# Two sparse graph-attention layers: another order of the first tiles' work, and edge places on GpSimd instead of VectorE

## The chip, the cores and the metric

The kernel runs on one core of a Trainium2 chip. The metric is the device time of one execution in microseconds. PE is TensorE, PEld its weight load, DVE VectorE, ACT ScalarE, POOL GpSimd and SP the engine that queues the plain DMAs. All times in this text are microseconds unless marked ns.

## The reference

Two graph-attention layers on 3327 nodes with 1024 features. `adj` is a symmetric 0/1 matrix with ones on its diagonal, with about 17 entries to a row. Cut to what matters:

```
# layer 0: 8 heads of 128
h = (x @ W).reshape(C, 8, 128)
e = leaky_relu(alpha_src[i] + alpha_dst[j], 0.2)      # alpha_* = sum over d of h * a_*
attn = softmax(where(adj == 0, -inf, e))              # over j
x = layernorm(x + attn @ h)
# layer 1: one head of 1024, the same form with W, a1, a2, and relu on its output
x = layernorm(x + relu(attn1 @ (x @ W1)))
```

## The kernel before

**Three stages.** Nodes are cut into 26 tiles of 128 rows (`NT`). The first part, which is all that the change touches, makes the features of layer 0 and turns the adjacency matrix into lists of edges. Then layer 0 gathers rows of `h0_d` by those lists, tile by tile, and layer 1 does the same with `y_d`. Between the first part and layer 0 a flag is computed that chooses the sparse branch; it needs the counts of all 26 tiles, so no gather starts before the first part is over.

**Features.** `flip(t)` transposes a tile of x on PE (L176) and copies it out on ACT (L179, two copies). `project(t, c)` multiplies it by the third `c` of W (8 values of k, each one product of fp32 in two passes, L480), and `keep(t, c)` copies the sum out on ACT (L497). The three thirds are 347, 347 and 346 columns wide. The last 16 columns of W are "W a", W times the attention vectors: they lie in third 2, so `project(t, 2)` needs them, and thirds 0 and 1 don't. For third 2, `keep` also makes `sd`, `r` and two exponentials on ACT (L492 to L495), and four small operations on POOL (`factors`, L296 to L299). The accumulators have two PSUM banks ("A"), so a project waits until the keep of the one two places before it has been done.

**W a.** `score_column(k)` makes it for rows 128k of W: products of W with `a_src` on DVE (L576) and with `a_dst` on POOL (L575), a sum over each head for the first on DVE (L577), and for the second either 8 sums on ACT (L582, columns 0 to 4) or one on DVE (L579, columns 5 to 7). The vectors reach all partitions by products with a row of ones (L560); the POOL's copy `av` is made from that by ACT (L563). The product tiles `pr0` and `pr1` have two buffers each.

**Edge lists.** For each tile:
- `count(t)`: POOL clears the diagonal in the mask (L308), ACT counts it (`junk`, L311), DVE packs its bytes (`words`, L318). Then POOL queues the load of a later mask. There are four mask buffers; `load_mask(t + 4)` takes the one that this very count reads, so that DMA waits on POOL's queue until the count is over.
- `ends` and `ends2`: a one-column product on PE (L327, L346), a copy on ACT (L328, L347), small operations on POOL (L335 to L353).
- `keys` and `columns`, in two halves each: DVE finds the 32 largest keys (L360, L274, L276) and unpacks them (L369 to L376), giving `pack`.
- `places`: ACT makes `away` (L385, L386); DVE casts `pack` to bf16, takes the remainder (L389, L390) and compares `away` with the degrees (L392, L393), which gives `place`.
- `give(0)` to `give(4)`: groups of small bf16 products on PE, with `place` as weights (L412, L402).
- `take`: six copies on ACT (L424 to L429). `sources`: DVE finds the gathered row of each place (L437 to L451).

**The order of the work** is written out by hand. `listing()` is a generator: each step emits one piece of list work. For tile t it yields four steps (`give(s)` of tile t with a half of `keys` or `columns` of tile t + 1), one step with `give(4)`, `take` and `count(t + 4)`, one with `sources`, and one with `places(t + 1)`, which is held back until third 2 of tile t + 1 has been kept. `pace()` is called after every second k of a project; it counts slots and emits as many steps as the ratio `7 * (NT + 1)` to `slots[1]` asks for. Before, 189 steps go to 284 slots, and a tile has 12 slots: a little under 8 steps for each tile of features, where 7 are a tile of lists. So the lists start behind and catch up. The main loop for t from 2 does `project(t, 0)`, `project(t, 1)`, `flip(t + 2)`, `project(t + 1, 2)`. Every engine runs its instructions in the order in which they were emitted.

```
while done[0] * slots[1] < slots[0] * (7 * (NT + 1)):
    done[0] += 1
    next(steps, None)
```

Of the kernel before, what the change touches and what calls it, by code (L numbers as in the profile page):

```python
# [26 lines left out]
def kernel(  # L27
# [125 lines left out]
    def spread(dst, a):  # L153

        nc.sync.dma_start(dst, bass.AP(tensor=a.tensor, offset=a.offset, ap=[[0, P], [1, D]]))

    class Phase:
# [74 lines left out]
        def edge_constants(self):  # L232
            self.io_w = self.iota([P, WD], [[1, WD]], "io_w")

            self.io_q = self.iota([P, EB * P], [[2 * P, EB], [2, P // 8], [P // 4, 8]], "io_q", base=1)
            part = self.pool.tile([P, 3, NB], I32, bufs=1, name="part")
            nc.gpsimd.iota(part[:, 0, NB - 1 :], pattern=[[0, 1]], base=0, channel_multiplier=1)
            for b in range(EB):
                for g in range(NG):
                    nc.gpsimd.iota(  # L240
                        part[:, 0, b * NG + g : b * NG + g + 1], pattern=[[0, 1]], base=(b + g) % EB * P,
                        channel_multiplier=1,
                    )
            nc.vector.tensor_scalar(
                part[:, 1, :], part[:, 0, :], 7, 4, op0=OP.bitwise_and, op1=OP.logical_shift_left
            )
            nc.vector.tensor_scalar(
                part[:, 2, :], part[:, 0, :], 3, 15, op0=OP.logical_shift_right, op1=OP.bitwise_and
            )

            nums = self.pool.tile([P, 1], I32, bufs=1, name="nums")
            nc.vector.tensor_scalar(nums, part[:, 0, NB - 1 :], GT - 1, None, op0=OP.bitwise_and)
            self.mvs = [self.pool.tile([P, 3, NY], BF16, bufs=1, name=f"mvs{n}") for n in range(4)]
            for mv in self.mvs:
                nc.vector.memset(mv, 0.0)
                nc.vector.tensor_scalar(mv[:, 0, :1], nums, 1.0, None, op0=OP.add)
                nc.vector.tensor_scalar(mv[:, 0, NY - 1 :], part[:, 0, NB - 1 :], 1.0, None, op0=OP.add)
            nc.vector.tensor_scalar(part[:, 0, :], part[:, 0, :], -P, None, op0=OP.bitwise_and)
            for n in range(2):
                nc.vector.tensor_tensor(part[:, 0, :], part[:, 0, :], part[:, n + 1, :], OP.bitwise_or)  # L260
            self.io_k = self.pool.tile([P, NB], F32, bufs=1, name="io_k")
            nc.vector.tensor_copy(self.io_k, part[:, 0, :])
            self.io_l = self.iota([P, KMAX], [[1, KMAX]], "io_l")
            self.bit = self.pool.tile([P, 8, KMAX], I32, bufs=1, name="bit")
            self.base = self.pool.tile([P, 8, KMAX], F32, bufs=1, name="base")
            for b in range(8):
                first = (b & 1) * NP // 2 + (b >> 1 & 1) * NP // 4 + (b >> 2) * NP // 8 + 1
                nc.vector.memset(self.bit[:, b, :], 1 << b)
                nc.vector.memset(self.base[:, b, :], float(first))

        def largest(self, dst, src, half):
# [8 lines left out]
    class Edges:  # L280
# [83 lines left out]
        def columns(self, half):  # L364

            sbuf, ph = self.ph.sbuf, self.ph
            if half == 0:
                ki = sbuf("ki", [P, 3, KMAX], 1, dt=I32)
                nc.vector.tensor_copy(ki[:, 0, :], self.top)  # L369
                nc.vector.tensor_scalar(ki[:, 1, :], ki[:, 0, :], 9, None, op0=OP.logical_shift_right)  # L370
                nc.vector.tensor_scalar(ki[:, 2, :], ki[:, 0, :], 511, None, op0=OP.bitwise_and)
                bits = sbuf("bits", [P, 8, KMAX], 1, dt=I32)
                nc.vector.tensor_tensor(bits, ki[:, 1:2, :].to_broadcast([P, 8, KMAX]), ph.bit, OP.bitwise_and)
                self.cols = sbuf("cols", [P, 8, KMAX], 1)
                nc.vector.tensor_tensor(self.cols, ki[:, 2:3, :].to_broadcast([P, 8, KMAX]), ph.base, OP.add)
                nc.vector.scalar_tensor_tensor(self.cols, bits, 0.0, self.cols, op0=OP.not_equal, op1=OP.mult)  # L376
                self.pack = sbuf("pack", [P, KMAX], 1)
            ph.largest(self.pack, self.cols.rearrange("p a b -> p (a b)"), half)

        def places(self):  # L380
# [5 lines left out]
            nc.scalar.activation(away[:, EB * P :], ph.io_q[:, :P], AF.Abs, bias=self.mid2, scale=-1.0)  # L386

            mv = self.mv = ph.mvs[self.t % 4]
            nc.vector.tensor_copy(mv[:, 0, XL:NX], pack)  # L389
            nc.vector.tensor_tensor(mv[:, 1, XL:NX], pack, mv[:, 0, XL:NX], OP.subtract)  # L390
            self.place = sbuf("place", [P, (EB + 1) * P], 2, dt=BF16)
            nc.vector.tensor_scalar(self.place[:, : EB * P], away[:, : EB * P], self.deg, None, op0=OP.is_lt)  # L392
            nc.vector.tensor_scalar(self.place[:, EB * P :], away[:, EB * P :], self.more, None, op0=OP.is_lt)  # L393

        def give(self, b):

# [35 lines left out]
        def sources(self):  # L432
# [1 line left out]
            sbuf, ph, t = self.ph.sbuf, self.ph, self.t  # L434
            xv, m = self.xs, NB - 1
            kq = sbuf("kq", [P, NB], 1)
            nc.vector.tensor_tensor(kq[:, :m], ph.io_k[:, :m], xv[:, :m, 0], OP.subtract)  # L437
            nc.vector.tensor_tensor(kq[:, m:], ph.io_k[:, m:], xv[:, m, KMAX + 1 :], OP.subtract)
            eq = sbuf("eq", [P, NB, KMAX], 1)
            nc.vector.tensor_tensor(  # L440
                eq, ph.io_l.unsqueeze(1).to_broadcast([P, NB, KMAX]),
# [12 lines left out]
    with ExitStack() as own, tc.manual_schedule():  # L454
# [47 lines left out]
        def count(t):  # L502
            if t < NT:
                lists[t].words(ads.pop(t), junk)
                load_mask(t + 4)

        def listing():

            for t in range(-1, NT):
                old, new = lists[t] if t >= 0 else None, lists[t + 1] if t + 1 < NT else None  # L510
                for s in range(4):
                    if old:
                        old.give(s)
                    if new:
                        (new.keys, new.columns)[s // 2](s % 2)
                    if s == 1 and t + 3 < NT:
                        lists[t + 3].ends(tri_b)
                    if s == 3 and t + 3 < NT:
                        lists[t + 3].ends2(all_b)
                    yield  # L520
                if old:
# [26 lines left out]
        arow = [pool.tile([1, D], F32, bufs=1, name=f"arow{n}") for n in range(2)]  # L548
        for n, a in enumerate((a0_src, a0_dst)):
            nc.sync.dma_start(arow[n], bass.AP(tensor=a.tensor, offset=a.offset, ap=[[D, 1], [1, D]]))  # L550
        for k in range(KT):
            nc.sync.dma_start(wt[:, k, :D], w0[k * P : (k + 1) * P, :])
            if k == 3:
                load_x(1)
        one = pool.tile([1, P], F32, bufs=1, name="one")
        nc.vector.memset(one, 1.0)
        avs = bank("S", [P, NG, HALF], "avs")
        for n in range(4):
            half = slice(n % 2 * HALF, (n % 2 + 1) * HALF)
            nc.tensor.matmul(avs[:, n, :], one, arow[n // 2][:, half], start=True, stop=True)  # L560
        av = pool.tile([P, D], F32, bufs=1, name="av")
        for n in range(2):
            nc.scalar.activation(av[:, n * HALF : (n + 1) * HALF], avs[:, 2 + n, :], AF.Copy)  # L563
        masks = [pool.tile([P, NP], U8, bufs=1, name=f"ad{n}") for n in range(5)]
        for ad in masks[:4]:
            nc.vector.memset(ad[:, N:], 0.0)
# [4 lines left out]
        def score_column(k):  # L571
            pr = [ph.sbuf(f"pr{n}", [P, D], 2) for n in range(2)]
            to = [wt[:, k, D + n * H : D + (n + 1) * H] for n in range(2)]
            heads = [pr[n].rearrange("p (h d) -> p h d", h=H) for n in range(2)]
            nc.gpsimd.tensor_tensor(pr[1], wt[:, k, :D], av, OP.mult)  # L575
            nc.vector.tensor_tensor(pr[0], wt[:, k, :D], avs[:, :2, :].rearrange("p a b -> p (a b)"), OP.mult)  # L576
            nc.vector.tensor_reduce(to[0], heads[0], AX.X, OP.add)  # L577
            if k > 4:
                nc.vector.tensor_reduce(to[1], heads[1], AX.X, OP.add)  # L579
                return  # L580
            for h in range(H):
                nc.scalar.activation(junk_h, heads[1][:, h, :], AF.Copy, accum_out=to[1][:, h : h + 1])  # L582

        flip(0)
        for k in range(3):
            score_column(k)
        load_mask(0)
        project(0, 0, False)
        keep(0, 0)
        flip(1)  # L590
        load_x(2)
        score_column(3)
        project(0, 1, False)
        keep(0, 1)
        score_column(4)
        load_mask(1)
        project(1, 0, False)
        for k in range(5, KT):
            score_column(k)
        keep(1, 0)  # L600
        project(1, 1, False)
        keep(1, 1)

        tri = pool.tile([P, P], F32, bufs=1, name="tri")
        nc.vector.memset(tri, 0.0)
# [4 lines left out]
        )  # L610
        tri_b = pool.tile([P, P], BF16, bufs=1, name="tri_b")
        nc.vector.tensor_copy(tri_b, tri)
        count(0)
        ph.edge_constants()

        nc.vector.memset(tri, 1.0)
# [2 lines left out]
        )  # L619
        all_b = pool.tile([P, P], BF16, bufs=1, name="all_b")  # L620
        nc.vector.tensor_copy(all_b, tri)
        lists[0].ends(tri_b)
        lists[0].ends2(all_b)
        load_mask(2)
        count(1)
        flip(2)
        load_x(3)
        slots[1] = (NT - 2) * 12 - 4
        project(0, 2, False)
        keep(0, 2)  # L630
        load_mask(3)
        count(2)
        lists[1].ends(tri_b)
        lists[1].ends2(all_b)
        flip(3)
        load_x(4)
        project(1, 2)
        keep(1, 2)
        project(2, 2)
        keep(2, 2)  # L640
        for t in range(2, NT):
            load_x(t + 3)
            if 4 <= t < 4 + KT:
                nc.sync.dma_start(wt1[:, t - 4, :], w1[(t - 4) * P : (t - 3) * P, :])
# [567 lines left out]
```

## Time and profile before

| | us |
|---|---|
| median of 10 runs (1908.44 to 1914.04) | 1911.33 |
| the profiled execution, its own time | 1915.67 |
| its span, first to last instruction | 1913.6 |
| PE busy over the span | 1512.4 |
| last product of the first part ends | 490 |
| first gather of layer 0 is issued | 497 |
| first gather of layer 1 is waited for | 1217 |

The profile's 40 slices are 47.8 us each, so the first part fills the first ten and a half. In a timeline line the columns are start, duration, engine, source line, operation, output and inputs, sizes and how many were merged; the bracket gives the idle time before it and who ended it. In a table of waits the columns are the total in us, how often, and the longest. A pass of a 128x346 product takes 0.295 us when PE runs without gaps, so a project of 16 passes takes 4.73.

### The profile page before, as it was taken

How to read it: one execution, taken by the hardware profiler on the slowest of the kernel's cores; microseconds unless marked ns; L12 is line 12 of the kernel's file. 1: busy time of each engine (PE TensorE's matmuls, PEld its weight loads, DVE VectorE, ACT ScalarE, POOL GpSimd, SP SyncE). 2: the span in 40 equal slices, each digit the busy share in tenths (PEclk: the TensorE clock that was granted, in tenths of full speed). 3: DMA queues.
4: the chain of work that ended last, by engine and by line, in shares of the span. 5: the costliest groups of instructions: out<-in, count | busy, mean ns of one | idle time of the engine just before them, and what ended most of it. 6: DMA issues, size and time to landing. Idle time of an engine off the chain costs nothing.

```text
span 1913.6 us, 38096 instructions
## 1 busy us (share of the span) xinstructions
PE 1512.4 (79%) x14663; PEld 897.7 (47%) x14663; DVE 1148.4 (60%) x3083; ACT 545.4 (29%) x1408; POOL 1038.7 (54%) x1393
## 2 busy tenths in 40 slices
PE   6699999999456566555566555399999999999997
PEld 3455555666345455454455544134444444444443
DVE  5599999888287566666566666344444444444442
ACT  5355554442112222222222222012221222222210
POOL 4322222211466667676676664577766676666650
PEclk9799999999668877787778878699999999999999
DMA  5655565411699999999999998799999999999980
GB/s 151 98 122 111 119 111 99 97 61 50 227 392 372 398 393 400 374 405 400 392 383 393 398 387 299 286 395 409 404 385 371 388 374 369 358 371 374 372 336 33
DMA packets 170923, 567.22 MB, mean 296 GB/s; under 512 B 27674, under 2 KB 34330, under 8 KB 170734
## 3 DMA queue, kind: packets, MB, share of 16 engines
q0 software_dynamic: 131056, 455.68, 67.3%
q1 hardware_dynamic: 39678, 109.04, 15.0%
q8 instruction: 117, 1.92, 0.4%
q14 instruction: 72, 0.59, 0.1%
HBM read 578.33 MB, written 42.97 MB: 325 GB/s over the span
## 4 chain that ended last, share of the span: by engine, by line
PE 54%; DMA 23%; DVE 11%; ACT 6%; issue 4%; POOL 3%; DVEq 0%; ACTq 0%; SPq 0%; POOLq 0%
DMA src<-h_d,idx 21%; PE mm L1005 19%; PE mm L480 13%; PE acc L973 12%; DVE e L850 3%; PE tr L176 3%; PE acc L878 3%; ACT junk L311 2%; POOL src L783 2%; DVE pr L911 1%; ACT xT L179 1%; PE acc L862 1%; DMA src<-y_d,idx 1%; PE xp L412 1%; DMA own<-h_d 1%
## 5 line engine op out<-in xcount | busy, mean ns | idle before, releaser
L783 POOL DMA_INDIRECT src<-h_d,idx x416 | 442.2, 1063 | 205.0 <-PE acc L878 60.1
L783 POOL DMA_INDIRECT src<-y_d,idx x416 | 416.5, 1001 | 221.3 <-PE acc L973 95.0
L878 PE MATMUL acc<-src,e 128*32 128x128 f32 x6656 | 275.9, 335 | 255.2 <-DVE e L850 254.9
L480 PE MATMUL mm<-wt,xT 128*128 128x347 f32 (+1 forms) x1248 | 399.2, 466 | 3.0 <-ACT xT L179 2.2
L1005 PE MATMUL mm<-wt,xT 128*128 128x512 f32 x832 | 381.6, 602 | 0.8 <-DVE o L1008 0.8
L878 PEld LDWEIGHTS acc<-src,e 128*32 128x32 f32 x6656 | 232.1, 136 | 313.9 <-DVE e L850 286.8
L480 PEld LDWEIGHTS mm<-wt,xT 128*128 128x128 f32 x1248 | 227.7, 192 | 106.3 <-ACT xT L179 3.0
L1005 PEld LDWEIGHTS mm<-wt,xT 128*128 128x128 f32 x832 | 151.6, 189 | 198.4 <-issue 178.0
L973 PE MATMUL acc<-src,es 128*32 128x342 f32 (+1 forms) x2496 | 205.7, 463 | 34.1 <-DVE es L964 32.3
L850 DVE TENSOR_TENSOR e<-oh,way 128x1024 f32<-128x1024 f32 x130 | 158.8, 1221 | 59.2 <-ACT w L848 58.8
L973 PEld LDWEIGHTS acc<-src,es 128*32 128x32 f32 x2496 | 71.5, 111 | 158.6 <-issue 113.1
L848 ACT ACTIVATE w<-way 128x32 f32<-128x32 f32 (+1 forms) x130 | 24.7, 190 | 402.5 <-DVE way L846 390.9
L1008 DVE SCALAR_TENSOR_TENSOR o<-mm,y 128x512 f32<-128x512 f32 x52 | 36.0, 692 | 163.6 <-PE mm L1005 163.6
L987 ACT ACTIVATE z<-y,ri 128x342 f32<-128x342 f32 (+1 forms) x78 | 39.5, 569 | 313.4 <-DVE ri L983 313.4
L845 DVE TENSOR_TENSOR way<-src,re 128x32 f32<-128x32 f32 x104 | 20.9, 201 | 175.1 <-DMA src<-h_d,idx 154.9
L179 ACT ACTIVATE xT<-tr 128x512 f32<-128x512 f32 x104 | 59.4, 595 | 140.4 <-PE tr L176 140.4
L961 DVE TENSOR_TENSOR way<-way,src 128x128 f32<-128x128 f32 x104 | 31.1, 299 | 95.0 <-DMA src<-y_d,idx 51.0
L311 ACT ACTIVATE junk<-ad 128x3328 uint8<-128x3328 uint8 x26 | 78.3, 3013 | 11.1 <-POOL ad L308 11.1
L830 ACT ACTIVATE own<-own,es 128x128 f32<-128x128 f32 x208 | 63.6, 388 | 59.7 <-DVE es L827 59.7
L862 PE MATMUL acc<-end,e 128*128 128x128 f32 x416 | 64.8, 319 | 13.6 <-DVE e L850 13.6
L870 PE MATMUL acc<-own,ident 128*128 128x512 f32 x104 | 62.0, 680 | 8.5 <-ACT own L830 8.5
L862 PEld LDWEIGHTS acc<-end,e 128*128 128x128 f32 x416 | 59.8, 229 | 15.9 <-DVE e L850 15.9
(190 smaller groups left out, 1857.4 us busy)
## 6 DMA issues: line engine op xcount, KB each, us to landing
h_d<-ht SPq DMA_DIRECT2D x26, 520.0 KB
own<-h_d SPq DMA_DIRECT2D x26, 520.0 KB
y_d<-y SPq DMA_DIRECT2D x26, 514.0 KB
y<-y_d SPq DMA_DIRECT2D x26, 514.0 KB
x<-in_x_dram SPq DMA_DIRECT2D x25, 512.0 KB
y<-in_x_dram SPq DMA_DIRECT2D x25, 512.0 KB
out_dram<-o SPq DMA_DIRECT2D x25, 512.0 KB
ad<-in_adj_dram POOLq DMA_DIRECT2D x25, 415.9 KB
```

What stands on the lines that cost most here:

```text
L176: nc.tensor.transpose(tr[:, k, :], src[:, (4 * g + k) * P : (4 * g + k + 1) * P], ident)
L179: nc.scalar.activation(part, tr, AF.Copy)
L311: nc.scalar.activation(junk, ad, AF.Copy, accum_out=self.deg)
L480: nc.tensor.matmul(acc, xT[t][:, k, :], wt[:, k, CUTS0[c] : CUTS0[c + 1]], start=k == 0, stop=k == KT - 1)
L783: nc.gpsimd.indirect_dma_start(out=s[:, g, :w], out_offset=None, in_=table[:, :], in_offset=bass.IndirectOffsetOnAxis(ap=idx[:, t, b * NG ...
L830: nc.scalar.activation(hn, hn, AF.Copy, scale=es[:, n : n + 1])
L850: nc.vector.tensor_tensor(e, oh.unsqueeze(2).to_broadcast([P, ng, H, wide]), wp.unsqueeze(3).to_broadcast([P, ng, H, wide]), OP.mult,)
L862: nc.tensor.matmul(self.acc[h // 4][:, h % 4, :], e[:, 0, h, :], rowsof[:, 0, h, :], start=False, stop=h % 4 == 3,)
L870: nc.tensor.matmul(self.acc[b - 1].rearrange("p h d -> p (h d)"), ident, self.h[:, (b - 1) * HALF : b * HALF], start=False, stop=False,)
L878: nc.tensor.matmul(self.acc[h // 4][g * GT : (g + 1) * GT, h % 4, :], e[:, g, h, :], rowsof[:, g, h, :], start=first and h % 4 == 0, stop= ...
L973: nc.tensor.matmul(self.acc[c][to, :m], es[:, g, :], s[:, g, CUTS[c] : CUTS[c + 1]], start=b == 0, stop=b == EB,)
L1005: nc.tensor.matmul(acc, xT[:, k, :], wt1[:, k, half], start=k == 0, stop=k == KT - 1)
```

## The change

All edits lie in the first part; layers 0 and 1 are not touched.

- **Start.** x tiles 1 to 4 are loaded a little earlier. `av` is loaded by a DMA that repeats one row to all partitions, ahead of W, and no longer copied by ACT. Columns 0 to 5 of W a have their second product on POOL and their second sums on ACT; columns 6 and 7 have both on DVE, which reads both vectors from PSUM.
- **Order of the first tiles.** Thirds 0 and 1 of tiles 0, 1 and 2 are done while W a is made, and then thirds 2. The constants for the edges now come ahead of `count(0)`. `keys` and `columns` of tile 0 are emitted between the projects, and the pacing starts with 4 steps done at slot 9, with 189 steps to 289 slots.
- **Masks.** `count(t)` now queues `load_mask(t + 3)`, into the buffer that the count before has read.
- **Places on POOL.** The cast and the remainder of `pack`, both comparisons that make `place`, and the two subtractions at the head of `sources` move from DVE to POOL. `pack` gets a second buffer.
- **Unpacking.** The bit masks are shifted by 9, so one DVE operation of `columns` goes.

```
-                nc.vector.memset(self.bit[:, b, :], 1 << b)
+                nc.vector.memset(self.bit[:, b, :], 512 << b)
...
             mv = self.mv = ph.mvs[self.t % 4]
-            nc.vector.tensor_copy(mv[:, 0, XL:NX], pack)
-            nc.vector.tensor_tensor(mv[:, 1, XL:NX], pack, mv[:, 0, XL:NX], OP.subtract)
+            nc.gpsimd.tensor_copy(mv[:, 0, XL:NX], pack)
+            nc.gpsimd.tensor_tensor(mv[:, 1, XL:NX], pack, mv[:, 0, XL:NX], OP.subtract)
...
-            nc.vector.tensor_scalar(self.place[:, : EB * P], away[:, : EB * P], self.deg, None, op0=OP.is_lt)
-            nc.vector.tensor_scalar(self.place[:, EB * P :], away[:, EB * P :], self.more, None, op0=OP.is_lt)
+            nc.gpsimd.tensor_scalar(self.place[:, : EB * P], away[:, : EB * P], self.deg, None, op0=OP.is_lt)
+            nc.gpsimd.tensor_scalar(self.place[:, EB * P :], away[:, EB * P :], self.more, None, op0=OP.is_lt)
...
-            nc.vector.tensor_tensor(kq[:, :m], ph.io_k[:, :m], xv[:, :m, 0], OP.subtract)
-            nc.vector.tensor_tensor(kq[:, m:], ph.io_k[:, m:], xv[:, m, KMAX + 1 :], OP.subtract)
+            nc.gpsimd.tensor_tensor(kq[:, :m], ph.io_k[:, :m], xv[:, :m, 0], OP.subtract)
+            nc.gpsimd.tensor_tensor(kq[:, m:], ph.io_k[:, m:], xv[:, m, KMAX + 1 :], OP.subtract)
...
             lists[t].words(ads.pop(t), junk)
-                load_mask(t + 4)
+                load_mask(t + 3)
```

The order of the first tiles, after the change (without the constants):

```
flip(0); score_column(0); score_column(1); load_mask(0)
project(0, 0, False); keep(0, 0); flip(1); load_x(3)
score_column(2); project(0, 1, False); keep(0, 1); score_column(3); load_mask(1)
project(1, 0, False); keep(1, 0); flip(2); load_x(4)
score_column(4); project(1, 1, False); keep(1, 1); score_column(5); load_mask(2)
project(2, 0, False); keep(2, 0); score_column(6); score_column(7)
...
count(0); next(steps); next(steps)
project(2, 1, False); keep(2, 1); project(0, 2, False); keep(0, 2)
lists[0].ends(tri_b); count(1); next(steps); next(steps)
project(1, 2, False); keep(1, 2)
lists[0].ends2(all_b); lists[1].ends(tri_b); count(2); flip(3); load_x(5)
done[0], slots[:] = 4, [9, (NT - 3) * 12 + 13]
project(2, 2); keep(2, 2); lists[1].ends2(all_b); lists[2].ends(tri_b)
flip(4); project(3, 2); keep(3, 2); lists[2].ends2(all_b)
for t in range(3, NT): ...
```

At the first slot of `project(2, 2)` the pacing emits three steps at once: `count(3)`, `places(0)`, and `give(0)` of tile 0 with a half of `keys(1)`. The order before:

```
flip(0); score_column(0); score_column(1); score_column(2); load_mask(0)
project(0, 0, False); keep(0, 0); flip(1); load_x(2)
score_column(3); project(0, 1, False); keep(0, 1); score_column(4); load_mask(1)
project(1, 0, False); score_column(5); score_column(6); score_column(7); keep(1, 0)
project(1, 1, False); keep(1, 1)
...
count(0)
...
lists[0].ends(tri_b); lists[0].ends2(all_b); load_mask(2); count(1); flip(2); load_x(3)
slots[1] = (NT - 2) * 12 - 4
project(0, 2, False); keep(0, 2); load_mask(3); count(2)
lists[1].ends(tri_b); lists[1].ends2(all_b); flip(3); load_x(4)
project(1, 2); keep(1, 2); project(2, 2); keep(2, 2)
for t in range(2, NT): ...
```

## The prediction

> **What bounds the kernel now.** I read the page's slices first.
>
> ```profile
> span 1913.6 us, 38096 instructions
> ...
> PE   6699999999456566555566555399999999999997
> ...
> DVE  5599999888287566666566666344444444444442
> ...
> PEclk9799999999668877787778878699999999999999
> ```
>
> The change touches only the first ten slices. There PE stands at 9 from the third slice on, and DVE at 8 to 9: one of the two, or a chain through both, sets the pace. PE's products are the same before and after, so I account for PE's lost time: idle, or at half clock. The timeline of PE at the start:
>
> ```profile
> 26.76 9.61 PE L480 MATMUL mm<-wt,xT 128*128 128x347 f32 x32 [2.21 <-ACT xT L179]
> 46.18 0.16 PE L327 MATMUL op<-deg_b,tri_b 128*128 128x1 bf16 x1 [9.81 <-ACT deg_b L313]
> 55.20 0.16 PE L346 MATMUL op<-more_b,all_b 128*128 128x1 bf16 x1 [8.86 <-POOL more_b L340]
> 55.30 1.94 PE L176 MATMUL tr<-ident,x 128*128 128x128 f32 x8
> 57.03 5.82 PE L480 MATMUL mm<-wt,xT 128*128 128x346 f32 x16
> ...
> 70.61 0.16 PE L346 MATMUL op<-more_b,all_b 128*128 128x1 bf16 x1 [7.76 <-POOL more_b L340]
> ...
> 72.45 4.31 PE L480 MATMUL mm<-wt,xT 128*128 128x346 f32 x8
> ...
> 86.60 0.24 PE L412 MATMUL xp<-mvs,place 32*128 32x42 bf16 x12 [0.30 <-DVE place L392]
> ```
>
> Lost here: 2.2 at 24.6; 18.8 from 36.4 to 55.2; 7.8 from 62.9 to 70.6. After each long gap PE runs slowly: transposes take 1.94 where 1.04 is usual, 16 passes 5.82 for 4.73, 8 passes 4.2 for 2.36: 2.0 and 2.8 lost. Sum 33.6.
>
> Then the waits from 80 to 330:
>
> ```profile
> PEld L412 <- DVE place L392: 18.2, 13, 2.1
> PE xp L412 <- DVE place L392: 9.5, 10, 1.5
> ...
> DVE place L392 <- ACT away L385: 5.8, 9, 2.3
> ...
> PE xp L412 <- POOL mvs L299: 1.5, 1, 1.5
> ...
> PE mm L480 <- ACT ht L497: 0.8, 2, 0.4
> ```
>
> PE's own waits are 9.5 + 1.5 + 0.8 = 11.8, nearly all at `give(0)`, for `place`. From 330 on PE has none (40.00 busy of 40). Is DVE the late one? One turn of the timeline says mostly no:
>
> ```profile
> 188.41 0.22 PE L402 MATMUL xp<-mvs,place 128*128 128x43 bf16 x3
> ...
> 189.62 3.02 ACT L311 ACTIVATE junk<-ad 128x3328 uint8<-128x3328 uint8 x1
> ...
> 192.87 0.17 ACT L492 ACTIVATE sd<-mm 128x16 f32<-128x16 f32 x1
> ...
> 193.62 0.73 ACT L385 ACTIVATE away<-io_q,place_of 128x512 f32<-128x512 f32 x1
> ...
> 194.39 0.48 DVE L392 TENSOR_SCALAR place<-away,cnt 128x512 bf16<-128x512 f32 x1 [0.74 <-ACT away L385]
> ...
> 194.93 0.24 PE L412 MATMUL xp<-mvs,place 32*128 32x42 bf16 x12 [1.53 <-DVE place L392]
> ```
>
> It is a loop: `give(4)` on PE, the copies and the 3 us count on ACT, whatever keep stands between, `away`, the comparison, `give(0)`. DVE itself waited 0.74 for `away`. So total lost before: 33.6 + 11.8 = 45.4.
>
> [...] the product of 128x1024 takes 2.37 on POOL (L575) and 1.21 on DVE (L576). It shows no large one-input comparison. [...] Here a small POOL cast (L296), 0.19 to 0.21 elsewhere, took 0.60 at 86.69 beside the two-input key operation of DVE. [...]
>
> **The change part by part.**
>
> *Start, up to W a.* ACT's queue decides. Its first copy is done at 14.3. A column's eight sums take 3.48 (15.37 to 18.81), a keep of a third 0.45, a pair of xT copies 1.07. Columns 0 and 1, keep, xT, column 2, keep, column 3 end at about 30.3; the next keep waits for PE till 31.1 (I grant PE 1.5 lost: `av` puts 0.5 MB ahead of W, and POOL, freed from waiting for ACT's `av`, issues the first mask's load near 13 instead of 21, beside W). Then keep, xT and column 4 end at 36.6, keep and column 5 at 40.8. DVE does columns 0 to 5 in 2.39 each from 12, but in column 6 its second product needs the `pr1` buffer of column 4, which ACT reads until 36.6, and in column 7 that of column 5. Each product or sum is 1.21: W a is ready at 45.0, against 41.5 before. Meanwhile PE has seven projects to do and isn't held: they end at 46.3, `project(0, 2)` at 51.1.
>
> *Constants and first count.* In the trace before, the stretch from the first table cast (47.33) to the end of the second triangle on POOL (53.80) is 6.5; with 1.6 ahead, and 0.3 for the diagonal, the count of tile 0 can start 8.4 after W a. It lasts 3.3 (42.82 to 46.13). So `deg_b` of tile 0 comes at 45.0 + 11.7 = 56.7. `keep(2, 1)` is queued behind that count, and `project(1, 2)` needs its bank: PE idles from 51.1 to 57.2, 6.1.
>
> *From there to the first `give(0)`* everything is a chain through ACT and POOL: keep(2, 1), keep(0, 2) and a copy 1.75; `ends` 1.75; diagonal 0.35; count 1 3.3; sd and r 0.45; factors 1.1; `ends2` 1.15; `ends` 1.5; diagonal 0.35; count 2 3.3; xT 1.1; count 3 3.3; away 0.75; comparison 0.8. Sum 21.0: `give(0)` at 77.7. PE's order puts only `project(1, 2)`, a flip and two products in front of it. Lost: 1.0 slow, 1.0 waiting for count 1, 0.5 slow, 11.3 idle, 2.2 slow afterwards (before: 2.0 and 2.8). Start in all: 1.5 + 6.1 + 1.0 + 1.0 + 0.5 + 11.3 + 2.2 = 23.6, against 33.6. Gain 10.0.
>
> *Places on POOL.* DVE loses 0.37 + 0.79 + 0.33 a tile of lists, and 0.17 by the unpacking. It took 15.5 a tile (from one `re` store to the next), so it falls to 13.9, under the 14.7 that pacing gives (7 steps are 10.7 slots, of 12 to a tile of 16.5). That removes DVE's share of PE's waits. But the ACT chain stays, and its end gets longer. The comparison of 128x512 on POOL: [...] I take 0.68, against 0.51 on DVE. [...] Where third 2 is kept between, POOL does the four factors first (1.5 after r), then cast and remainder (0.55), then compares. The mask's DMA, which held POOL's queue until the count was over, no longer does: without that edit these would queue behind it. The subtractions for `sources` now wait on POOL's queue for `take`; behind them stand only the factors and places of the next tile, which come later anyway.
>
> *PE's waits, counted.* With T the start of `give(4)`: `away` starts at T + 4.45 with no keep between, + 4.79 with one, + 5.75 with keep and xT, + 5.21 with third 2 (all read from the timeline). `place` follows 1.30 later on DVE, 1.50 on POOL; with third 2 on POOL at T + 7.29. PE arrives at T + 4.96 after 8 products, 6.15 after 10, 7.34 after 12; with a flip, 5.86 and 7.05. On the order of before this rule gives 8.8, against 11.0 measured for `give(0)`; the rest is DVE. On the order after, tile by tile: 2 with third 2 and 8 products, 2.33 each; 5 with third 2 and 10, 1.14; 2 with xT and 8, 1.39; 3 with xT and 10, 0.20; 1 with a keep and 8, 1.33; 3 with a keep and 10, 0.14; 2 with none and 8, 0.99; 1 with none, 8 and a flip, 0.09; the last two, without a count, 0.6 each. Sum 18.8. The new ratio, 189 to 289, also ends the catching up at tile 20 instead of 15, so the waits last longer. Loss against 11.8: 7.0.
>
> *Tail.* The last `give(4)` ends the projects as before; the subtractions on POOL add 0.4 (two of 0.2 and a hop). DMAs: masks and x are loaded tiles ahead, nothing waits.
>
> **Sum.** 23.6 + 18.8 = 42.4 for 45.4, and 0.4: -2.6. Span 1913.6 - 2.6 = 1911.0, own time 1915.67 - 2.6 = 1913.1; the median was 4.3 below that execution, 1911.33, so 1908.7: 1909.
>
> **Rivals.**
> *DVE was the bound* (faster). DVE stands at 9 in these slices, and PE's waits name it. If POOL's end of the loop costs no more than DVE's (0.5, and POOL's factors overlap the count), the rule gives 10.0 instead of 18.8: -11.4, 1900. For it: DVE's 94% busy. Against: DVE waited for `away` 9 times of 16.
> *POOL's comparison is the new wait* (slower). It stands between `away` and `give(0)`, and above 0.75 PE waits for it in 24 of 25 tiles, so each 0.1 costs about 2.4. At 1.07 the waits are 28, and the kernel +6.8: 1918. It decides from 0.79 (level with before); at 0.95 the kernel is slower by 0.2%. [...] For it: [...] the 0.60 cast. Against: at that moment DVE should be in MAX8, beside which POOL's operations keep to 0.19.
> *The start gains nothing*: had the chain to `give(0)` 10 more, the end would be +7.4, 1919; every row in it is measured, so I give it little.
>
> **How the numbers follow.** A measurement here tells about 0.2%, 3.8 us, from no change. The forecast's case, 1904 to 1914, has 0.45; the faster rival 0.27; the slower, with the dearer start, 0.28. Within the forecast's case some 0.17 lies beyond -3.8 and 0.03 beyond +3.8: faster 0.44, same 0.25, slower 0.31. The range runs from 1899 to 1921.
>
> **What would show it.** W a ready near 45 with DVE waiting on ACT's sums; first `give(0)` near 78; PE's waits for `place` near 19 in all, released by POOL; a comparison of 0.68; no wait of PE on DVE. Wrong if `give(0)` comes before 73 or after 83, or the comparison is below 0.5 or above 0.95.

## The result, and the profile after

| | before | after |
|---|---|---|
| median of the runs | 1911.73 (28 runs) | 1958.94 (8 runs, 1956.25 to 1962.35) |
| the profiled execution, its own time | 1915.67 | 1957.88 |
| its span | 1913.6 | 1955.4 |
| W a ready | 41.5 | 50.0 |
| first `give(0)` | 86.6 | 83.8 |
| waits of PE for `place` at `give(0)` from there on (without the first `give(0)` itself) | 9.2 in 9 | 45.5 in 25 |
| mean of a pass of features from there on | 0.3184 | 0.3351 |
| start of the last feature product (below: the mark) | 489.5 | 536.8 |

After against before the ratio is 1.0246 (95% interval 1.0237 to 1.0255): 47 us slower. The forecast was 1909, in a range that ended at 1921. The two marks differ by 47.3, so the whole loss lies in the first part; layers 0 and 1 took 5.5 less in the profiled execution of after (span less mark is 1418.6 against 1424.1).

The same slices as before, from the page of the changed kernel:

```profile
span 1955.4 us, 38076 instructions
...
PE   8688989989936666555556655389999999999997
...
DVE  4677777876538666666666665434444444444442
...
PEclk9799989999967888777788887689999999999999
```

The reader is to see three things. DVE has fallen from 8 and 9 to mostly 7 in slices 3 to 10, as the change means it to. PE has not risen with it: it has an 8 in places where there were only nines. And the first part fills eleven slices, not ten. So relieving DVE did not quicken PE.

The start on PE, from the timeline, and after it the waits from 80 to 330:

```profile
18.77 0.85 PE L479 MATMUL mm<-wt,xT 128*128 128x347 f32 x2 [0.43 <-DMA wt<-in_L_gnn_W_dram]
22.91 1.53 PE L479 MATMUL mm<-wt,xT 128*128 128x347 f32 x2 [3.29 <-DMA wt<-in_L_gnn_W_dram]
...
61.62 0.16 PE L327 MATMUL op<-deg_b,tri_b 128*128 128x1 bf16 x1 [5.05 <-ACT deg_b L313]
...
70.24 1.09 PE L176 MATMUL tr<-ident,x 128*128 128x128 f32 x8 [1.02 <-ACT cnt L328]
```

```profile
PEld L411 <- POOL place L391: 46.8, 14, 11.9
...
DVE wd L318 <- POOL ad L308: 43.6, 12, 10.1
PE xp L411 <- POOL place L391: 39.1, 14, 11.3
...
POOL place L391 <- ACT away L384: 32.8, 9, 4.4
...
DVE eq L439 <- POOL kq L437: 14.5, 9, 4.5
```

Where there stood `PE xp L412 <- DVE place L392: 9.5` there is now POOL, with 39.1. Two waits of DVE on POOL have grown: for the diagonal (L308) from 5.4 in one to 43.6 in 12, and for `kq` (the output of the two subtractions) from nothing to 14.5. What POOL needs for the comparison is in the view of its line:

```profile
L391 POOL TENSOR_SCALAR place<-away,cnt x26: 1561/1576/2116, 81.7 to 527.1; 128x512 bf16<-128x512 f32 x26
...
  PE xp L411: 56.8, 26
```

Minimum, median and maximum are in ns: 1.58 us, where I had taken 0.68 and, in the dearest case that I priced, 1.07. PE waited for it in all 26 tiles.

How the 47.3 add up: the first `give(0)` comes 2.8 earlier; the waits behind it grow by 45.5 - 9.2 = 36.3; the passes behind it take 373.7 - 359.2 = 14.5 more, though 12 fewer are left to do there; what remains is -0.7.

### The profile page after: what moved, and what is told of

Same layout as the page of the kernel before. It is cut to its first block, busy times and chain, and to the rows that moved or that the text cites. A ratio compares the mean times of both kernels' runs of the same rounds, so it can differ in the third digit from the quotient of the medians.

```text
span 1955.4 us, 38076 instructions
## 1 busy us (share of the span) xinstructions
PE 1533.4 (78%) x14663; PEld 906.4 (46%) x14663; DVE 1119.0 (57%) x2902; ACT 546.7 (28%) x1422; POOL 1119.6 (57%) x1547
## 4 chain that ended last, share of the span: by engine, by line
PE 51%; DMA 22%; ACT 8%; DVE 8%; POOL 6%; issue 4%; DVEq 0%; POOLq 0%; ACTq 0%; SPq 0%
DMA src<-h_d,idx 20%; PE mm L1023 19%; PE acc L991 12%; PE mm L479 11%; ACT junk L311 4%; DVE e L868 3%; PE acc L896 3%; PE tr L176 2%; POOL place L391 2%; POOL src L801 2%; DVE pr L929 1%; ACT xT L179 1%; PE acc L880 1%; DMA wt<-in_L_gnn_W_dram 1%; PE xp L411 1%
## 5 line engine op out<-in xcount | busy, mean ns | idle before, releaser
L479 PE MATMUL mm<-wt,xT 128*128 128x347 f32 (+1 forms) x1248 | 419.9, 484 | 4.4 <-DMA wt<-in_L_gnn_W_dram 3.7
L479 PEld LDWEIGHTS mm<-wt,xT 128*128 128x128 f32 x1248 | 236.5, 199 | 119.5 <-issue 15.3
L1023 PEld LDWEIGHTS mm<-wt,xT 128*128 128x128 f32 x832 | 151.6, 189 | 198.4 <-issue 178.0
L991 PE MATMUL acc<-src,es 128*32 128x342 f32 (+1 forms) x2496 | 207.0, 465 | 32.1 <-DVE es L982 32.1
L991 PEld LDWEIGHTS acc<-src,es 128*32 128x32 f32 x2496 | 71.7, 111 | 157.0 <-issue 113.3
L391 POOL TENSOR_SCALAR place<-away,cnt 128x512 bf16<-128x512 f32 x26 | 43.0, 1655 | 48.6 <-ACT away L384 48.6
```

Source lines behind the costliest of these rows:

```text
L391: nc.gpsimd.tensor_scalar(self.place[:, : EB * P], away[:, : EB * P], self.deg, None, op0=OP.is_lt)
L479: nc.tensor.matmul(acc, xT[t][:, k, :], wt[:, k, CUTS0[c] : CUTS0[c + 1]], start=k == 0, stop=k == KT - 1)
L991: nc.tensor.matmul(self.acc[c][to, :m], es[:, g, :], s[:, g, CUTS[c] : CUTS[c + 1]], start=b == 0, stop=b == EB,)
L1023: nc.tensor.matmul(acc, xT[:, k, :], wt1[:, k, half], start=k == 0, stop=k == KT - 1)
```

## The experiments

**The theories.** A: the comparison on POOL, far dearer than estimated, stands between `away` and `give(0)`. B: the new order, pacing and mask loads cost it. C: the small operations in POOL's queue (cast, remainder) cost it. Later ones are named where they come up. The kernels ran on several chips, on some of which layers 0 and 1 took longer: span less mark is 1418.6 to 1433.0 in the six traces from the chips on which before had medians of 1911.7 and 1919.0, and 1472.4 to 1507.6 in the ten from those on which it had 1971.8 to 1993.5. So a ratio is always to the kernel before on the same chip, and across chips I compare the mark, which ends ahead of the layers: kq_early and start_only, from two such chips, have marks 0.2 apart. A mark is read from one trace of each kernel, and how far it scatters was not measured. "Waits after it" are PE's waits for `place` at `give(0)`; compare_dve has 3.2 more there, and first_piece_dve 4.5, for the cast and the remainder on POOL.

| kernel | ratio to before (95%) | first `give(0)` | waits after it | mean pass after it | mark |
|---|---|---|---|---|---|
| before | 1 | 86.6 | 9.2 | 0.3184 | 489.5 |
| after | 1.0246 (1.0237, 1.0255) | 83.8 | 45.5 | 0.3351 | 536.8 |
| compare_dve | 1.0081 (1.0057, 1.0105) | 80.4 | 17.5 | 0.3255 | 498.5 |
| places_dve | 1.0044 (1.0028, 1.006) | 80.7 | 20.6 | 0.3255 | 498.1 |
| start_only | 0.996 (0.995, 0.997) | 81.1 | 10.7 | 0.3215 | 483.6 |
| places_pool | 1.0189 (1.0166, 1.0211) | 87.8 | 36.6 | 0.3257 | 525.9 |
| compare_cut | 1.0048 (1.002, 1.0077) | 79.2 | 23.0 | 0.3253 | 498.4 |
| kq_early | 0.998 (0.9964, 0.9996) | 80.9 | 10.9 | 0.3214 | 483.8 |
| mended | 1.0038 (1.0019, 1.0056) | 82.6 | 19.2 | 0.3241 | 497.0 |
| kq_dve | 1.0185 (1.0168, 1.0202) | 83.8 | 40.6 | 0.3333 | 530.0 |
| first_piece_dve | 0.9983 (0.997, 0.9997) | 81.4 | 6.7 | 0.3214 | 485.6 |
| b_count_later | 0.9974 (0.9958, 0.999) | 86.4 | 6.1 | 0.3179 | 482.9 |
| start_count_later | 0.9896 (0.9859, 0.9932) | 79.5 | 2.7 | 0.3211 | 473.4 |
| mended_count_later | 1.0265 (1.023, 1.0301) | 79.1 | 2.5 | 0.3374 | 547.1 |
| start_mask_later | 0.9946 (0.9928, 0.9963) | 76.3 | 10.9 | 0.3217 | 479.1 |
| start_count_mask_later | 0.9876 (0.9848, 0.9903) | 72.6 | 2.6 | 0.3208 | 466.1 |

### compare_dve, places_dve, start_only: putting the operations back

compare_dve:

```
-            nc.gpsimd.tensor_scalar(self.place[:, : EB * P], away[:, : EB * P], self.deg, None, op0=OP.is_lt)
-            nc.gpsimd.tensor_scalar(self.place[:, EB * P :], away[:, EB * P :], self.more, None, op0=OP.is_lt)
+            nc.vector.tensor_scalar(self.place[:, : EB * P], away[:, : EB * P], self.deg, None, op0=OP.is_lt)
+            nc.vector.tensor_scalar(self.place[:, EB * P :], away[:, EB * P :], self.more, None, op0=OP.is_lt)
```

> The changed kernel with only the two comparisons that make place back on VectorE; cast, remainder and the two subtractions stay on GpSimd. Theory A (the comparison's time on GpSimd, 1.66 us where 0.68 was assumed, stands in the loop give(4), count, away, comparison, give(0), and its long waits also put TensorE to half clock): the comparison goes from 1.66 to 0.5, some 24 times 1.1 us and most of the slow passes come back: 1915 to 1925, TensorE's waits for place under 20 us. Rival B (the loss is in the new order of the first tiles and the new pacing, not in the engine): stays above 1940. Rival C (GpSimd is too busy as a whole, the many small operations delay the masks' diagonal): 1930 to 1945, with waits of ScalarE on L308 left.

places_dve has the cast and the remainder of `pack` on DVE too, start_only also the two subtractions for `kq`:

```
-            nc.gpsimd.tensor_tensor(kq[:, :m], ph.io_k[:, :m], xv[:, :m, 0], OP.subtract)
-            nc.gpsimd.tensor_tensor(kq[:, m:], ph.io_k[:, m:], xv[:, m, KMAX + 1 :], OP.subtract)
+            nc.vector.tensor_tensor(kq[:, :m], ph.io_k[:, :m], xv[:, :m, 0], OP.subtract)
+            nc.vector.tensor_tensor(kq[:, m:], ph.io_k[:, m:], xv[:, m, KMAX + 1 :], OP.subtract)
```

> The changed kernel with all four operations of places back on VectorE (cast, remainder, two comparisons); only the subtractions of sources stay on GpSimd. Theory A: no more than 3 us from the run with the comparisons alone, 1908 to 1920, since cast and remainder matter only where third 2 is kept in between. Rival B: above 1940. Rival C: clearly better than the run with the comparisons alone, by over 8 us.

> The changed kernel with nothing of the list work on GpSimd that was not there before: start, order, pacing and masks are as after the change. Theory A: 1906 to 1914, about level with the kernel before: the start loses 30 us of TensorE in the trace after the change against 34 before, and the waits for place go on a tile or four longer. Rival B: within 10 us of the changed kernel, above 1945.

The comparisons give back 38.3 of the mark (536.8 to 498.5), the `kq` subtractions 14.5 (498.1 to 483.6), and cast and remainder 0.4. The times of compare_dve and places_dve differ by 7.9, but their marks by 0.4: C looked nearly right by the time alone and is not, for the rest lies in layers 0 and 1, which none of the edits touches: the two traces are 4.0 apart at the first product of layer 1's sums (L991) and 8.5 at their ends. B falls: start_only keeps order, pacing and masks, and is 5.9 ahead of before at the mark (the mask loads cost something, below, but less than the order gains). A is right in the main, but compare_dve lies above A's 1915 to 1925, and still does with the 7 us taken off by which the kernel before was slower on that chip (1919.0 for 1911.7): `kq` was in no theory.

### places_pool: the four places operations alone, in the kernel before

```
-            nc.vector.tensor_copy(mv[:, 0, XL:NX], pack)
+            nc.gpsimd.tensor_copy(mv[:, 0, XL:NX], pack)
...
-            nc.vector.tensor_scalar(self.place[:, : EB * P], away[:, : EB * P], self.deg, None, op0=OP.is_lt)
+            nc.gpsimd.tensor_scalar(self.place[:, : EB * P], away[:, : EB * P], self.deg, None, op0=OP.is_lt)
```

(and the same for the remainder and the second comparison)

> The kernel before with only the four operations of places moved to GpSimd, nothing else. Theory A: the comparison takes 1.6 us there too, and the mask's DMA now holds it back behind the count as well; 20 times 1.2 to 1.9 us and slow passes: 1945 to 1965. Rival B: 1908 to 1920, as before.

36.4 later at the mark, and the comparison is 1.58 (median) here too. This part of the change makes most of the loss by itself.

### compare_cut: is it the time to the first place, or POOL's load?

```
-            nc.gpsimd.tensor_scalar(self.place[:, : EB * P], away[:, : EB * P], self.deg, None, op0=OP.is_lt)
+            for b in range(EB):
+                r = slice(b * P, (b + 1) * P)
+                nc.gpsimd.tensor_scalar(self.place[:, r], away[:, r], self.deg, None, op0=OP.is_lt)
```

> The changed kernel with its 128x512 comparison still on POOL, but cut into four of 128x128 (0.62 us each in the changed kernel's trace, so 2.5 us for the four where the one took 1.58): more work on POOL, but give(0) needs only the first piece, give(1) the second, and so on. Theory A, latency: what costs is the time from away to the first place that PE can use. It falls by about 0.95 us in each of 26 runs of the steps, 25 us, and some half-clock passes with it: 1920 to 1938 on a chip where the kernel before takes 1912 to 1919. Rival D, occupancy: what costs is how much work stands in POOL's queue. POOL gets 0.9 us more per run and the kernel is level with the changed one or slower, 1955 to 1975.

```profile
L393 POOL TENSOR_SCALAR place<-away,cnt x104: 597/617/1158, 78.1 to 491.4; 128x128 bf16<-128x128 f32 x104
...
  PE xp L413: 33.3, 22
```

POOL now compares for 4 x 0.617 = 2.47 a tile and not 1.58, and the kernel is 38.4 faster at the mark, as fast as with all comparisons on DVE. The cost was latency: `give(0)` needs a quarter of the result and waited for all of it. D falls.

### kq_early: why do two operations of 0.2 cost 14.5?

In places_dve, a turn with third 2 kept between (POOL and DVE, from the timeline; xs is complete at 218.5):

```profile
222.50 0.19 POOL L296 CAST mvs<-r 128x8 bf16<-128x8 f32 x1 [3.88 <-ACT r L295]
...
223.31 0.21 POOL L299 TENSOR_TENSOR mvs<-r,mvs 128x8 bf16<-128x8 f32 x1
223.47 0.23 POOL L436 TENSOR_TENSOR kq<-io_k,xs 128x16 f32<-128x16 f32 x1
...
223.88 0.72 DVE L439 TENSOR_TENSOR eq<-io_l,kq 128x544 f32<-128x544 f32 x1 [4.22 <-POOL kq L437]
...
226.85 0.48 DVE L391 TENSOR_SCALAR place<-away,cnt 128x512 bf16<-128x512 f32 x1
```

The factors of the next tile are emitted before `sources`. They need `r`, which stands behind the 3 us count on ACT, so POOL waits 3.88 with `kq` queued behind it; DVE waits 4.22 for `kq`; and DVE's comparison is queued behind the whole of `sources`. On DVE, in a like turn of start_only, `xs` is complete at 250.55, and `kq` follows behind the packing of a mask (L318), while ACT still counts until 253.87:

```profile
251.62 0.18 DVE L436 TENSOR_TENSOR kq<-io_k,xs 128x16 f32<-128x16 f32 x1
```

The edit of kq_early only issues the two operations ahead of the factors:

```
                 count(t + 4)
+                if old:
+                    old.offsets()
                 yield
...
+        def offsets(self):
...
+            kq = self.kq = sbuf("kq", [P, NB], 1)
+            nc.gpsimd.tensor_tensor(kq[:, :m], ph.io_k[:, :m], xv[:, :m, 0], OP.subtract)
+            nc.gpsimd.tensor_tensor(kq[:, m:], ph.io_k[:, m:], xv[:, m, KMAX + 1 :], OP.subtract)
```

(places as in places_dve)

> The changed kernel with the four places operations on VectorE (as in places_dve, 1927.0) and kq still on POOL, but the two kq operations are issued right after the count, ahead of the next tile's factors. Nothing is faster, only the order in POOL's queue differs. Theory E, order of the queue: kq costs because POOL's factors, which wait 4 us for the edge scores that stand behind the count on ScalarE, are queued ahead of it; with kq ahead of them the time falls to that of start_only, 1909 to 1916 (ratio 0.995 to 1.000 to the kernel before). Rival F, price and hop: kq costs because two operations on POOL and the hand-over to VectorE take longer than on VectorE; then the time stays at 1923 to 1930.

DVE's waits for `kq` from 80 to 330, in places_dve and then in kq_early:

```profile
DVE eq L439 <- POOL kq L437: 10.6, 5, 4.5
...
DVE eq L444 <- POOL kq L436: 1.0, 2, 0.5
```

The mark is 483.8, start_only's 483.6: on POOL `kq` costs next to nothing by itself. It was the place in the queue. F falls.

### mended, kq_dve, first_piece_dve: do the two losses add?

mended is the changed kernel with both rearrangements, the cut and the early `kq`.

> The changed kernel with every operation left on the engine that the change gave it, and two rearrangements together: the 128x512 comparison on POOL in four pieces of 128x128 (as in compare_cut) and kq issued ahead of the next tile's factors (as in kq_early). The mark is the start of the last feature product of the first part: 489.5 us in the kernel before, 536.8 in the changed one, 498.4 in compare_cut, 483.8 in kq_early, 483.6 in start_only. If the two losses are separate, as theory A with E has it, the mark comes to that of start_only, 482 to 487, and the ratio to the kernel before to 0.995 to 0.999. If they hide behind each other, or the longer queue of POOL counts after all, the mark stays at 492 to 500 and the ratio at 1.001 to 1.006.

They don't: 497.0, hardly better than compare_cut alone. So I tried `kq` on DVE with all the places on POOL (the second diff above), and mended with the first piece on DVE:

```
             for b in range(EB):
                 r = slice(b * P, (b + 1) * P)
-                nc.gpsimd.tensor_scalar(self.place[:, r], away[:, r], self.deg, None, op0=OP.is_lt)
+                engine = nc.gpsimd if b else nc.vector
+                engine.tensor_scalar(self.place[:, r], away[:, r], self.deg, None, op0=OP.is_lt)
```

> The changed kernel with the two kq operations on VectorE and the four places operations left on POOL. With the places on VectorE, kq on POOL cost 14.5 us of the mark (483.6 to 498.1). Theory J, the two losses are separate: the mark falls by as much, from 536.8 to 520 to 525. Rival K, kq's cost was that the sources of the last tile stood ahead of the comparison in VectorE's queue; with the comparison on POOL only the two kq operations themselves (0.4 us) stand ahead of it, in some ten runs of the steps: mark 530 to 536, and the loss of the changed kernel is the comparison on POOL nearly alone.

> The kernel `mended` (comparison in four pieces, kq ahead of the factors; mark 497.0) with the first of the four pieces on VectorE and the other three, the 128x128 for the last product and the cast and remainder on POOL. Theory L: what is left of the loss is that the first piece stands behind POOL's other work (factors, cast, remainder) and takes 0.62 us there: mark 483 to 487, as with all of it on VectorE. Rival M: the later pieces, or what stands behind them in POOL's queue, hold up the work: mark 492 to 497.

kq_dve gains 6.8: `kq` costs 14.5 where the comparison stands behind `sources` on DVE, and 6.8 (at the lower edge of K's 530 to 536) where it stands on POOL. The loss divides as 38 + 14.5 or as 46 + 7, by which is put back first; neither split is the true one. A turn of the changed kernel shows both in one chain:

```profile
258.18 3.02 ACT L311 ACTIVATE junk<-ad 128x3328 uint8<-128x3328 uint8 x1
...
261.90 0.19 POOL L296 CAST mvs<-r 128x8 bf16<-128x8 f32 x1 [3.87 <-ACT r L295]
...
262.18 0.73 ACT L384 ACTIVATE away<-io_q,place_of 128x512 f32<-128x512 f32 x1
...
262.88 0.23 POOL L436 TENSOR_TENSOR kq<-io_k,xs 128x16 f32<-128x16 f32 x1
...
263.49 0.63 POOL L389 TENSOR_TENSOR mvs<-pack,mvs 128x32 bf16<-128x32 f32 x1
264.11 2.11 POOL L391 TENSOR_SCALAR place<-away,cnt 128x512 bf16<-128x512 f32 x1
264.12 0.74 DVE L443 TENSOR_TENSOR eq<-eq,xs 128x544 f32<-128x544 f32 x1
...
266.28 0.23 PE L411 MATMUL xp<-mvs,place 32*128 32x42 bf16 x12 [3.20 <-POOL place L391]
...
266.44 1.43 PE L479 MATMUL mm<-wt,xT 128*128 128x347 f32 x4
268.02 2.65 PE L479 MATMUL mm<-wt,xT 128*128 128x347 f32 x4
```

`away` is done at 262.91. POOL is at the factors, then `kq`, then cast and remainder, and compares from 264.11 on. PE waits 3.20 in all, and a little later, at a granted clock of 0.50 (268.1 to 271.3), four passes take 2.65 where the four before took 1.43.

first_piece_dve, 485.6, comes within 2.0 of start_only with three quarters of the comparison still on POOL: what mended had left was the time to the first piece, behind POOL's other work. M falls.

### b_count_later, start_count_later, mended_count_later: is ACT's count the loop?

```
-                count(t + 4)
                 yield
...
                     new.places()
+                count(t + 4)
+                if new:
                     yield
```

b_count_later is this in the kernel before, start_count_later in start_only, mended_count_later in mended (there `kq` is issued where the count was).

> The kernel before with one move: the count of tile t+4 (3.4 us of ScalarE, with its halving on VectorE and its mask load) is issued after the places of tile t+1 and not before the sources of tile t. Theory A (the wait at give(0) is ScalarE's count ahead of away): away starts some 3.4 us earlier, the waits of PE for place in the loop (11.8 us) go to 0 to 3, and the half-clock passes after them: 8 to 13 us less, ratio 0.993 to 0.996. If those waits are set by something else (VectorE's queue ahead of the comparison, or the ends that the moved count feeds come late): level, ratio 0.998 to 1.003, with as long a wait under another name.

> start_only (the changed kernel with places and kq all on VectorE, ratio 0.996 to the kernel before) with the count issued after the places. Theory A: the 10 us that PE waits for place after the first run, and the half-clock passes after them, go: 8 to 12 us less than start_only, ratio 0.990 to 0.992, 1893 to 1900 us where the kernel before takes 1912. If the count matters only because of something queued behind it that is still late: level with start_only, 0.995 to 0.997.

> The kernel `mended` with the count issued after the places, and kq where the count was. If theory A holds as it did for start_count_later (mark 473.4, ratio 0.990), away starts 3.4 us earlier also here: mark 472 to 477, ratio 0.989 to 0.992, and VectorE's share of the first part is smaller at the same time, with no gain from that. If the smaller work of VectorE is worth something once the waits are gone, the mark is below that of start_count_later, 468 to 472.

Before, the waits fell from 9.2 to 6.1 and the mark by 6.6, less than the 8 to 13 expected (there were no slow passes to win back: the mean granted clock of before is 1.00 from the first `give(0)` to the mark); in start_only they fell from 10.7 to 2.7 and the mark by 10.2, as expected. So ACT's count is in the loop, but in the kernel before DVE's queue stands close behind it, as a turn of b_count_later shows:

```profile
157.24 0.71 ACT L385 ACTIVATE away<-io_q,place_of 128x512 f32<-128x512 f32 x1
...
159.18 0.18 DVE L451 SCALAR_TENSOR_TENSOR idx<-v 128x17 int32<-128x17 f32 x1
...
159.59 0.48 DVE L392 TENSOR_SCALAR place<-away,cnt 128x512 bf16<-128x512 f32 x1
...
160.13 0.24 PE L412 MATMUL xp<-mvs,place 32*128 32x42 bf16 x12 [0.94 <-DVE place L392]
```

`away` is done at 157.95, and DVE comes to the comparison 1.64 later, behind `sources` of the tile before (L437 to L451). From 80 to 330 DVE waits for `away` once, where it waited 9 times. The same move in mended lost 50.1. There the count needs the diagonal, which POOL clears (L308) and which is now queued behind POOL's pieces: in one turn they end at 267.6, and ACT, idle for 3.94, starts to count at 267.88. The waits of mended_count_later from 80 to 330:

```profile
ACT junk L311 <- POOL ad L308: 50.2, 14, 5.0
...
PE op L327 <- ACT deg_b L313: 28.0, 12, 3.0
```

PE hardly waits for `place` any more (2.5 in all), but for the counts. An order that is good for one assignment of engines can be bad for another.

### start_mask_later, start_count_mask_later: the rest of the start

```
         score_column(1)
-        load_mask(0)
...
         score_column(3)
-        load_mask(1)
+        load_mask(0)
...
         score_column(5)
+        load_mask(1)
         load_mask(2)
```

> start_only with the first mask load issued after score column 3 and the second after score column 5, so that neither moves beside W's rows. Theory G: the first mask, which the change issues before the first products, takes the DMA engines from W's last row, which so lands at 22.9 us and not at some 17 to 18; without it PE's wait of 3.3 to 3.8 us for that row goes, W a is complete 3 to 5 us earlier and so is the first place: the mark (483.6 in start_only) 478 to 481, ratio 0.9930 to 0.9950. Rival H: the start is bound by the score products themselves or by the masks, which come later now: PE waits as long elsewhere, mark 482 to 486, ratio 0.9955 to 0.9975.

> start_count_later with the first two masks loaded later as in start_mask_later: all that has been found to gain, and nothing of what was found to lose. If the two gains are separate (theory G right): mark 468 to 471, ratio 0.9865 to 0.9890. If theory G is wrong: as start_count_later, mark 472 to 475, ratio 0.989 to 0.991.

The start on PE in start_mask_later:

```profile
20.02 0.85 PE L479 MATMUL mm<-wt,xT 128*128 128x347 f32 x2 [0.44 <-DMA wt<-in_L_gnn_W_dram]
...
55.70 0.16 PE L327 MATMUL op<-deg_b,tri_b 128*128 128x1 bf16 x1 [5.06 <-ACT deg_b L313]
...
76.35 0.27 PE L411 MATMUL xp<-mvs,place 32*128 32x42 bf16 x12 [9.72 <-DVE place L391]
```

The wait for W's last row falls from 3.75 (in start_only) to 0.44, the first `give(0)` from 81.1 to 76.3, the mark by 4.5. G is right, H falls. Both gains together give 466.1, 23.4 ahead of before, a little more than I expected (468 to 471), and a ratio of 0.9876: the fastest kernel of the study. Its places and `kq` are on DVE.

## Why the prediction was wrong

**The step that failed: the price of the comparison, "I take 0.68".** It is 1.58, above even the dearest case that I priced ("At 1.07 the waits are 28"). Both figures were my estimates, and no measured row stood behind them: the trace of before shows no large one-input comparison on POOL. A straight line through the two sizes, 1.576 for 512 elements and 0.615 for 128, gives, as an estimate, 2.50 ns an element and 0.295 for the operation besides. The trace of before had a warning in it that I quoted and did not use: POOL's product of 128x1024 takes 2.37, which is 2.3 ns an element with two inputs. Half of that, 1.19, was the nearest row for 512 elements, above my dearest case and above the 0.79 to 0.95 from which I had said that "slower" decides. A measured row of the same engine should have been one end of the range. In the terms of the sum: the waits were to cost 7.0 more and cost 36.3 more, slow passes behind them were to cost nothing and cost 14.5, and the first `give(0)` was to come 8.9 earlier and came 2.8 earlier.

**The rule for the waits held.** "Each 0.1 costs about 2.4": 0.90 more is 21.6, and 18.8 + 21.6 = 40.4. kq_dve, in which of the moved work only the places are on POOL, measures 40.6, and 22 of its 24 waits lie between 0.7 and 3.1. On DVE the rule gave 10.0, start_only measures 10.7. So the loop through `give(4)`, ACT and `away` was read rightly, and the slower rival had the right place and mechanism, at too low a price. The faster rival, "DVE was the bound", does not hold as the main bound: after relieved DVE and lost, and start_only and the kernels made from it gained with DVE's work put back. But DVE comes next: of the 9.2 of waits, 6.1 were left when the count was out of the way (b_count_later), and DVE, which hardly waited for `away` any more, ended them.

**What the sum left out.** The waits were priced as idle time alone. The mean pass after the first `give(0)` went from 0.3184 to 0.3351, 0.0167 on 1116 passes: 18.6. From there to the mark the mean granted clock is 1.00 before and 0.96 after, and 0.04 of the 453.1 is about 18: these are passes at half clock (0.50 granted). The trace of after has the half clock for 6.7 at the beginning and then nine times for 3.4, and each of the nine begins within 1.8 of the end of a wait of 1.9 to 4.0. Three waits of 1.9 to 2.3 have none beside them. Between 240 and 320, where waits of 2.0 to 3.2 stand, the mean is 0.91; start_only, whose waits are at most 1.5, has 1.00 there. I had counted slow passes only at the start, where the clock of before is 0.50 from 38.6 to 59.0 and from 66.0 to 76.0. That the slowdown comes from the waits is argued from this, not tried apart.

**`kq`: "behind them stand only the factors and places of the next tile, which come later anyway".** Wrong. The factors are emitted ahead of `sources`, so they stand in front of `kq`; I looked at what is behind the moved operation and not at what is ahead of it. Price 7 to 14.5. The 0.4 that it was to cost at the tail was right: the last wait ahead of the flag's transposes grew from 4.13 to 4.63.

**The start: "gain 10.0".** The first `give(0)` was to come at 77.7 and came at 83.8. W a was late, 50.0 for 45.0: I had granted PE 1.5 for the mask's load beside W, and PE waited 3.29 + 0.43 for W's rows, was at half clock for the rows that followed (0.50 from 22.3 to 29.0), and the whole chain moved with it (start_mask_later, without the mask beside W, has W a at 44.1 and takes 4.8 off start_only's first `give(0)`). From W a to `deg_b` it is 11.6 (forecast 11.7), from there to `give(0)` 22.2 (21.0; the comparison took 2.03 in that tile, where I had 0.8 with its hop, which is as much as the difference). DVE did wait for ACT's sums ahead of column 6, as said.

**No wait of PE on DVE**: right. **DVE to 13.9 a tile**: 15.5 was the distance between two turns, not DVE's busy time. Over the 25 turns from the first `give(0)` to the mark DVE was busy for 357.0 and is for 321.7, so 14.3 and 12.9 a turn: 1.4 less, where 1.66 was foreseen. The fall is there, and it gained nothing. (Its share fell further, 58.3 of 80 for 73.9 between 160 and 240, since the turns are longer.)

## What to carry to other kernels

Before an operation is moved to another engine, find the loop that sets the pace, and ask whether the operation is on it: then its latency on the new engine counts in full, however busy the old one was (in kq_dve against start_only the comparison takes 1.58 for 0.49, and the waits of 25 tiles 40.6 for 10.7). Price it from a measured row of the new engine and let that row be one end of the range. List what is queued ahead of each moved operation as well as behind it; and where a consumer needs only a part of a result, cutting the producer can be worth as much as a faster engine (498.4 and 498.5 here).

## What the runs showed of the hardware that was not expected

- A one-input comparison on POOL costs at least as much for each element as a two-input product: 2.50 ns (the estimate from two sizes, above) against 2.3 ns (2.37 for 128x1024). 128x512 took 1.58 on POOL and 0.49 on DVE, 128x128 took 0.615 and 0.28.
- The same comparison took 2.03 to 2.12 in four of 26 tiles. Three of the four ran beside DVE's `eq` product, its reduction and L447 (in the turn shown from 264.11 on), the first beside L372 to L375 of `columns` for 1.47 of its 2.03. The other 22 took 1.56 to 1.58 and ran, but for 0.03 of one of them, beside DVE's search for the largest keys (MAX8 and what belongs to it) or beside nothing. Whether these operations lengthen it was not tried apart. In the turn shown a small operation of DVE was longer too: L447 took 0.60 beside the comparison, where it takes 0.17 in places_dve. In before, POOL's cast L296, at a median of 0.198, took 0.60 in three of 26 tiles, each time mostly beside DVE's L360. The four long comparisons are not the cause of the loss, for the other 22 took more than twice the 0.68 too.
- A mask of 416 KB issued while W's last rows were under way delayed them by some 3.3 at PE (a wait of 3.75 in start_only, 0.44 in start_mask_later).
